# A two-layer graph kernel: first inputs of three pairs loaded at once, weights relaid, a replanned order

## The chip, the cores and the metric

The kernel runs on one core of a Trainium2 chip. TensorE (PE in the profile) multiplies matrices, VectorE (DVE) and ScalarE (ACT) work elementwise, GpSimd (POOL) does a few small operations, and SyncE (SP) issues nearly all transfers (DMA). Each engine takes its instructions in the order in which the program holds them, and waits on semaphores for what other engines or transfers must have finished. The metric is the device time of one execution in microseconds (us), lower is better. Before the change three runs took 2926.58, 2936.07 and 2936.2 us, median 2936.07 us.

## The reference, cut to what matters

There are 64 graphs of 256 nodes with 256 features each; everything is float32. Layer 0 is twice a graph attention, then a feed-forward part; layer 1 is an attention with 8 heads whose weights are masked by relation, then a feed-forward part.

```python
def gat(h, adj, W, a):                       # layer 0, twice
    Wh = h @ W
    e = leaky_relu(Wh @ a[:256] + (Wh @ a[256:]).T, 0.2)
    return softmax(where(adj > 0, e, NEG), axis=1) @ Wh
h = layernorm(x + gat(gat(x, ...), ...))
h = layernorm(h + relu(h @ w_ff1 + b_ff1) @ w_ff2 + b_ff2)
q, k = h @ Wq + bq, h @ Wk + bk              # layer 1, 8 heads of 32
attn = softmax(q @ k.T / sqrt(32))
out = sum((attn * (adj == r)) @ (h @ Wv[r] + bv[r]) for r in range(4))
h = layernorm(h + out @ Wo + bo)
return layernorm(h + gelu(h @ W1 + b1) @ W2 + b2)
```

## The kernel before

Two graphs make a pair, and 32 pairs run through the same way (`whole_way`, a generator): the two graph attentions (`gat_layers`), feed-forward, attention, feed-forward, store. Several pairs are in flight at once. The order of all instructions is made by a planner while the program is written, in `run`. It keeps a clock for each engine, takes the next step of a generator when TensorE's clock says that its inputs, its PSUM banks (eight) and its buffers are there, and queues the work of the other engines through `put`, which gives it a duration, a `lag` until others may read its result, and a rank. `keep_order` then fixes that order for each engine. So a planned duration changes no instruction; it changes where each one stands in its engine's queue. `START` gives the clocks at which the planner lets each engine begin, `landed` when it believes groups of weights to have arrived, and `CHANGES` changes ranks, degrees and orders at set times of TensorE's clock. `HURRIED` pairs (the first two) turn their attention rows by TensorE instead of through DRAM.

The start is written by hand. The lines up to L191 fold the two weight matrices of graph attention into `w12`: DVE forms four columns (L181), TensorE multiplies, and DVE copies the two halves out. `load` then brings a pair's three inputs: `xT` (512 KB, for the first product), `adjT` (512 KB of integers, made bytes by ACT at L390 and reduced by DVE at L394) and `x` (512 KB, for the residual). Pair 0 comes before the weights and pair 1 behind the first feed-forward weights. Their `adjT` lie in the buffer of the later values `v`; both pairs' `xT` share the one buffer `input`, and so does every transfer of a later pair's `xT` and `adjT`, so that pair 2's `adjT` waits for pair 1's first product, and its `xT` for that `adjT` to be read.

In `gat_layers` a first product (L166 over `input`) gives `xw`, which ACT evacuates (L650); ACT makes exponentials (L582 to L584), TensorE turns them into rows (L595) that ACT copies (L598); DVE weighs with the adjacency (L630, L632, one instruction each per half graph); ACT scales `xw` by the reciprocal sums (L639), and TensorE aggregates (L166 over `xw,e`). This is done twice. The name `gat` is held by one pair until its second product is done, so the next pair's first product waits for that.

Between these, `reliefs` takes the constant parts of biases out of the weights: one-column products (L1170) for the first feed-forward, for q and k, and for the second feed-forward, and then sums of weight blocks on DVE (L446, L440), since many products are done in seven block products instead of eight. These need the weights, which arrive in 28 transfers for six large matrices alone, cut as the blocks are used, in runs of 512 bytes to 2 KB.

Of the kernel before, what the change touches and what calls it, by code (L numbers as in the profile page):

```python
# [26 lines left out]
HURRIED = 2  # L27
SEVEN = (0, 2)
# [3 lines left out]
    (27.0, ("all", "slack", 0.2), ("rank", "means", 0)),  # L32
    (117.0, ("rank", "means", 1)),
    (207.0, ("all", "qkv", ("a1", "b1", "b2", "a2", "a6", "a5", "b6", "a7", "a4", "b5", "b7", "a3", "b4", "s0", "b3", "s1")),
     ("rank", "adj", 1), ("rank", "normalise", 2), ("rank", "exp", -1)),
    (297.0, ("degree", "fill", 1), ("all", "groups", (([0], []), ([1], []), ([], [2]), ([], [3]), ([2], []), ([3], []))),
     ("degree", "first", -1), ("all", "slack", 0.3)),
    (387.0, ("degree", "fill", 2.5), ("all", "slack", 0.8), ("rank", "mask", 1.5), ("rank", "turn", 2),
     ("all", "first", ("a1", "b1", "a6", "a2", "b2", "b6", "a5", "a7", "b7", "a4", "b5", "b4", "a3"))),
    (477.0, ("all", "slack", 0.1)),  # L40
    (657.0, ("rank", "qk", 2), ("rank", "adj", 0), ("rank", "act", 0.5), ("rank", "last", 0.5)),
    (1197.0, ("rank", "invert", 1.5), ("rank", "adj", -1), ("rank", "exps", -0.5),
     ("all", "first", ("a1", "b1", "a2", "a6", "b2", "b6", "a5", "a7", "b7", "a4", "b5", "b4", "a3")),
     ("rank", "normalise", 0), ("degree", "rows", 2)),
    (1287.0, ("rank", "turn", 1)),
    (1377.0, ("all", "groups", (([0], []), ([1], []), ([], [2]), ([], [3]), ([2], []), ([3], []))), ("rank", "divide", 1.5),
     ("rank", "copies", -2), ("all", "flight", 5)),
    (1467.0, ("all", "first", ("a1", "b1", "a2", "a6", "b2", "b6", "a5", "a7", "b7", "b5", "a4", "b4", "a3")),
     ("rank", "addends", 0.5)),
    (1557.0, ("rank", "copies", 1), ("rank", "qk", -2)),  # L50
    (1827.0, ("rank", "copies", -2)),
    (1917.0, ("rank", "v", 1)),
    (2007.0, ("rank", "rows", 1.5), ("rank", "squares", -0.5), ("rank", "copies", 0)),
    (2367.0, ("rank", "last", 1), ("rank", "adj", -0.5), ("degree", "attention", 0)),
    (2547.0, ("rank", "divide", 1), ("rank", "mask", 3)),
    (2637.0, ("degree", "first", 2.5)),
    (2727.0, ("rank", "last", 3), ("rank", "second", 0.5)),
    (2817.0, ("all", "first", ("a1", "b1", "a2", "a6", "b2", "b6", "a5", "a7", "b7", "b5", "a4", "b4", "a3")),
     ("rank", "second", -0.5), ("rank", "rows", -2)),
# [12 lines left out]
START = {"tensor": 8.5, "vector": 8.0, "scalar": 4.0, "gpsimd": 0.0, "sync": 32.0}  # L72
# [3 lines left out]
def two_layers(ctx: ExitStack, tc: tile.TileContext, t: dict, out: bass.AP, flag: bass.AP):  # L76
# [98 lines left out]
    nc.sync.dma_start(right[:, :, :D], t["L0_gnn_W2"].rearrange("(c p) m -> p c m", p=P))  # L175
    nc.scalar.dma_start(a2, bass.AP(tensor=t["L0_gnn_a2"].tensor, offset=t["L0_gnn_a2"].offset, ap=[[0, P], [1, 2 * D]]))
    nc.sync.dma_start(w1T, t["L0_gnn_W1T"].rearrange("(c p) m -> p c m", p=P))
# [7 lines left out]
    for columns in (slice(0, D), slice(D, D + 4)):  # L185
        for m in range(KC):
            for c in range(KC):
                by_strips(both[m][:, columns], lhsT=w1T[:, c, m * P:(m + 1) * P], rhs=right[:, c, columns],
                          start=c == 0 and columns.start == 0, stop=c == KC - 1, skip_group_check=True)
    for m in range(KC):  # L190
        nc.vector.tensor_copy(w12[:, m], both[m][:, :D + 4])  # L191
# [15 lines left out]
    free = {name: [0.0] * n for name, n in (("bank", 8 - KEPT), ("kept", KEPT), ("a", HQ), ("m", HQ), ("h", HQ), ("yb", 1), ("yT", 2), ("yTa", 1),  # L207
# [15 lines left out]
    def put(engine, us, emit, *events, rank=1, lag=0.2, kb=0, function=None, needs=None, frees=(), event=None, behind=None):  # L223
# [46 lines left out]
    def took(us):  # L270

        clock["tensor"] += us
        return at_time(clock["tensor"] + 0.2)
# [14 lines left out]
    def run(besides, ways):  # L288
# [12 lines left out]
        while True:  # L301
# [42 lines left out]
            else:  # L344
# [6 lines left out]
                clock[engine] += piece["us"]  # L351
# [15 lines left out]
    def load(pair, at=None):  # L367
# [4 lines left out]
        def adjT():  # L372
            if at is not None:
                to["adjT"] = work.tile([P, 2, 2, 2 * D], F32, name="v")[:, pair].bitcast(I32).rearrange(
                    "p b (c n) -> p (b c) n", c=2)
            else:
                to["adjT"] = io.tile([P, 4, N], I32, name="input")
            nc.sync.dma_start(to["adjT"], t["adjT"][rows].rearrange("b (c p) n -> p (b c) n", p=P))

        def xT():  # L380
            to["xT"] = io.tile([P, KC, 512], F32, name="input")
            nc.sync.dma_start(to["xT"], t["xT"][pair].rearrange("(c p) b n -> p c (b n)", p=P))
# [20 lines left out]
        if at is None:  # L403
            adj = in_bytes(there(adjT, needs="input"))
            return to, [there(xT, adj), adj, there(x, needs="x")]
        takes("input", pair == 0)
        takes("x")
        for emit in (xT, adjT, x):
            emit()
        return to, [at_time(at), in_bytes(at_time(at)), at_time(at)]  # L410

    def first_weights(name, wide=None):

        w = t[name]
        rows = w.shape[1] // 2
        s = const.tile([P, 7, rows], F32, name="w_" + name)
        for c, at in ((0, (0, 2)), (1, (1, 6))):
            for half, n in enumerate(at):  # L420
                nc.sync.dma_start(s[:, n], w[c * P:(c + 1) * P, half * rows:(half + 1) * rows])
# [9 lines left out]
    def last_weights(name):  # L431

        s = const.tile([P, 7, NF // 2, P], F32, name="w_" + name)
        for c, h, at in ((1, 0, 0), (0, 0, 1), (0, 1, 2), (1, 1, 3)):
            nc.sync.dma_start(s[:, at], t[name][c * FF // 2:(c + 1) * FF // 2, h * P:(h + 1) * P].rearrange("(k p) d -> p k d", p=P))
        return s

    def last_sums(w, there, event):
        for to, a, b in ((4, 3, 0), (5, 2, 4), (6, 2, 3), (3, 1, 5)):
            there = put("vector", 0.6, lambda to=to, a=a, b=b: nc.vector.tensor_tensor(w[:, to], w[:, a], w[:, b], ALU.subtract),  # L440
                        there, rank=5, event=event if to == 3 else None)
# [203 lines left out]
    def gat_layers(pair, to, loads):  # L645
        yield loads[:1], ["gat"], 2
        y = work.tile([P, 4, D + 4], F32, name="xw", bufs=2)
# [15 lines left out]
        frees_at(clock["tensor"], ["input"] * (pair > 0))  # L663
# [3 lines left out]
        for b in range(2):  # L667
            yield [e[b][1], *([] if b or not pair else [through_gat[pair - 1]])], None, 2
            if b == 0:
                z = work.tile([P, 4, D + 4], F32, name="xw", bufs=2)  # L670
# [7 lines left out]
        done_with("gat")  # L678
# [3 lines left out]
        for b in range(2):  # L682
# [7 lines left out]
            frees_at(there.time, ["e"])  # L690
# [437 lines left out]
    def layernorm_weights(g, beta, more=None):  # L1128
# [5 lines left out]
        return on_all(g, D), on_all(beta, D), more  # L1134

    landed = {name: at_time(us) for name, us in (("ln0", 8.0), ("ff0", 15.0), ("attention", 30.0), ("ff1", 37.0))}
    loaded = {0: load(0, 6.5)}
    ln = [layernorm_weights("L0_gnn_g_ln1", "L0_gnn_b_ln1", "L0_gnn_b_ff2")]
    ff0 = (first_weights("L0_gnn_w_ff1p"), column("L0_gnn_b_ff1"), (last_weights if 0 in SEVEN else weights)("L0_gnn_w_ff2"), Event())
    loaded[1] = load(1, 18.0)  # L1140
    ln.append(layernorm_weights("L0_gnn_g_ln2", "L0_gnn_b_ln2", "L1_gnn_bo"))

    wqk, wv = (const.tile([P, 7, D], F32, name=n) for n in ("wqk", "wv"))
    for n, name in enumerate(("L1_gnn_Wqp", "L1_gnn_Wkp")):
        for half, c, at in ((0, 0, 0), (0, 1, 1), (1, 0, 2), (1, 1, 6)):
            nc.sync.dma_start(wqk[:, at, n * P:(n + 1) * P], t[name][c * P:(c + 1) * P, half * P:(half + 1) * P])
    for r, c, at in ((0, 0, 0), (0, 1, 1), (1, 0, 2), (1, 1, 6)):
        nc.sync.dma_start(wv[:, at], t["L1_gnn_Wvp"][r, c * P:(c + 1) * P, :])
    bqk = const.tile([P, 2, KC], F32, name="bqk")
    for n, name in enumerate(("L1_gnn_bq", "L1_gnn_bk")):  # L1150
# [3 lines left out]
    ln.append(layernorm_weights("L1_gnn_g1", "L1_gnn_beta1", "L1_gnn_b2"))  # L1154
    ff1 = (first_weights("L1_gnn_W1p"), column("L1_gnn_b1"), (last_weights if 2 in SEVEN else weights)("L1_gnn_W2"), Event())
    ln.append(layernorm_weights("L1_gnn_g2", "L1_gnn_beta2"))
    biased = [put("vector", 0.4, lambda gbm=gbm: nc.vector.tensor_tensor(gbm[1], gbm[1], gbm[2][0], ALU.add), landed[name])
              for gbm, name in zip(ln, ("ln0", "attention", "attention"))]
    differences = [put("vector", 0.4, lambda to=to, of=of: nc.vector.tensor_tensor(to, to, of, ALU.subtract), landed["attention"])
                   for to, of in ((wv[:, 2], wv[:, 0]), (wv[:, 6], wv[:, 1]), (bv[:, D:], bv[:, :D]))]  # L1160
    relieved, through_gat = [Event() for _ in range(3)], [Event() for _ in range(NPAIR)]
# [21 lines left out]
    def reliefs():  # L1183
# [3 lines left out]
        if 0 in SEVEN:  # L1187
            last_sums(ff0[2], relieved[0], ff0[3])
# [13 lines left out]
        if 2 in SEVEN:  # L1202
            last_sums(ff1[2], relieved[2], ff1[3])
# [427 lines left out]
_BY_TRANSPOSED_ROWS = ("L0_gnn_w_ff1", "L1_gnn_Wq", "L1_gnn_Wk", "L1_gnn_Wv", "L1_gnn_W1")  # L1631
_ROWS_AND_COLUMNS = ("L0_gnn_b_ff2", "L1_gnn_bo", "L1_gnn_b2")

# [30 lines left out]
```

## Time and profile before

| | |
|---|---|
| median of three runs | 2936.07 us |
| the profiled execution's own time | 2928.64 us |
| its span in the profile | 2926.9 us |
| TensorE busy | 2874.6 us, 98% |
| DVE busy | 2629.6 us, 90% |
| ACT busy | 1847.4 us, 63% |
| mean granted TensorE clock | 0.993 |
| transfers | 211.84 MB, 72 GB/s on average |

The profile's rows by stretch of time give, for each engine, its busy microseconds and how many instructions these were; `PEclk` is the share of full clock granted to TensorE, and `DMA share` how busy the 16 transfer engines were. A row of the timeline has start, duration, engine, line, operation and tiles, and in brackets how long the engine had stood idle and what ended it. A matmul row's count is twice the program's for float32 data[...]. `PEld` is the load of the stationary operand.

### The profile page before, as it was taken

The numbers are of one execution on the slowest core, as the hardware profiler recorded it, in microseconds if no ns is written. First come the engines' busy times: TensorE is split into PE (matmuls) and PEld (weight loads), VectorE is DVE, ScalarE is ACT, GpSimd is POOL, SyncE is SP. The second block draws the span as 40 slices with busy tenths as digits, with TensorE's granted clock in tenths as the row PEclk, the third lists the DMA queues.
The fourth block names the chain that finished last, engine by engine and source line by source line (L and its number), as shares of the span: only waits on it lengthen the run. The fifth ranks groups of instructions, "written<-read, shape, count | busy, mean of one in ns | idle before, by whom it ended". The sixth has DMA issues, their size and how long they took to land. (4 is left out here: it accounts for less than half of the span.)

```text
span 2926.9 us, 147784 instructions
## 1 busy us (share of the span) xinstructions
PE 2874.6 (98%) x66066; PEld 2062.1 (70%) x66066; DVE 2629.6 (90%) x5874; ACT 1847.4 (63%) x5120; POOL 274.1 (9%) x518
## 2 busy tenths in 40 slices
PE   7999999999999999999999999999999999999998
PEld 4766776776776667766777767678767788677676
DVE  6899999899998889989998998999999999998887
ACT  4667666657656566565666665666666666665655
POOL 0010000100100001010100010010010000110001
PEclk8999999999999999999999999999999999999999
DMA  6222212222212222122222222221222222222100
GB/s 190 68 74 79 68 53 79 85 85 61 79 60 71 84 66 82 59 76 82 71 72 69 74 82 76 67 79 64 82 75 81 66 78 68 77 73 65 36 10 25
DMA packets 214178, 211.84 MB, mean 72 GB/s; under 512 B 22944, under 2 KB 173088, under 8 KB 213536
## 3 DMA queue, kind: packets, MB, share of 16 engines
q1 hardware_dynamic: 213120, 202.06, 22.0%
q8 instruction: 520, 8.52, 1.2%
q14 instruction: 122, 1.00, 0.1%
q10 hardware_dynamic: 416, 0.26, 0.0%
HBM read 137.51 MB, written 64.73 MB: 69 GB/s over the span
## 5 line engine op out<-in xcount | busy, mean ns | idle before, releaser
L166 PE MATMUL ps<-w_L_gnn_w_ff,ff 128*32 128x128 f32 x14336 | 426.9, 273 | 2.1 <-issue 1.4
L166 PEld LDWEIGHTS ps<-w_L_gnn_w_ff,ff 128*32 128x32 f32 x14336 | 397.3, 110 | 36.3 <-issue 13.0
L166 PE MATMUL ps<-w_L_gnn_W,ff 128*32 128x128 f32 x14336 | 418.3, 273 | 2.2 <-DVE qk L1091 0.9
L166 PEld LDWEIGHTS ps<-w_L_gnn_W,ff 128*32 128x32 f32 x14336 | 393.8, 110 | 30.6 <-issue 5.6
L1046 ACT ACTIVATE a<-ps 128x512 f32<-128x512 f32 x512 | 265.8, 600 | 145.7 <-PE ps L1037 145.0
L166 PE MATMUL ps<-yT,w_L_gnn_w_ff1p 128*32 128x256 f32 x5120 | 321.4, 382 | 10.8 <-ACT xw L650 10.6
L920 DVE TENSOR_TENSOR ff<-ff 128x1024 f32<-128x1024 f32 x256 | 311.2, 1215 | 16.0 <-PE ps L166 12.6
L738 POOL TENSOR_SCALAR rstd<-squares 128x2 f32<-128x2 f32 x256 | 78.2, 306 | 2625.1 <-ACT unread L733 2622.5
L733 ACT ACTIVATE unread<-x,less 128x256 f32<-128x256 f32 x512 | 259.6, 507 | 99.6 <-DVE less L708 68.6
L166 PE MATMUL ps<-yT,w_L_gnn_W1p 128*32 128x256 f32 x5120 | 316.0, 379 | 1.3 <-ACT ff L845 0.5
L845 ACT ACTIVATE ff<-ps 128x512 f32<-128x512 f32 x384 | 221.7, 588 | 146.5 <-PE ps L166 145.1
L1050 DVE TENSOR_TENSOR m<-a,adj 128x1024 f32<-128x1024 f32 x256 | 306.0, 1215 | 1.0 <-ACT a L1046 1.0
L517 DVE TENSOR_TENSOR ff<-ps,ff 128x512 f32<-128x512 f32 x384 | 260.2, 682 | 31.9 <-PE ps L166 20.4
L166 PE MATMUL ps<-xw,e 128*32 128x258 f32 (+1 forms) x4096 | 248.9, 385 | 5.8 <-ACT xw L639 5.8
L166 PEld LDWEIGHTS ps<-yT,w_L_gnn_w_ff1p 128*32 128x32 f32 x5120 | 172.6, 110 | 113.6 <-ACT xw L650 13.5
L166 PEld LDWEIGHTS ps<-yT,w_L_gnn_W1p 128*32 128x32 f32 x5120 | 171.9, 110 | 100.1 <-ACT ff L845 5.7
L851 ACT ACTIVATE ff<-ff,c_L_gnn_b_ff 128x256 f32<-128x256 f32 x384 | 172.8, 502 | 101.5 <-DVE ff L517 101.0
L917 DVE TENSOR_TENSOR x<-ps,x 128x256 f32<-128x256 f32 (+1 forms) x384 | 191.8, 504 | 33.8 <-PE ps L166 30.4
L166 PEld LDWEIGHTS ps<-xw,e 128*32 128x32 f32 x4096 | 138.4, 111 | 90.7 <-ACT xw L639 8.5
L739 POOL TENSOR_TENSOR rstd<-rstd,mhalf 128x2 f32<-128x2 f32 x256 | 195.2, 763 | 21.3
L851 ACT ACTIVATE ff<-ff,c_L_gnn_b 128x256 f32<-128x256 f32 x384 | 172.3, 504 | 36.8 <-DVE ff L517 35.5
L1007 ACT ACTIVATE qk<-ps,bqk 128x256 f32<-128x256 f32 x256 | 109.3, 468 | 118.3 <-PE ps L166 117.3
(133 smaller groups left out, 5091.7 us busy)
## 6 DMA issues: line engine op xcount, KB each, us to landing
home<-yb SPq DMA_DIRECT2D x182, 256.0 KB, 2.2
yT<-home SPq DMA_DIRECT2D x728, 64.0 KB, 2.1
rows<-row SPq DMA_DIRECT2D x60, 512.0 KB, 4.1
input<-in_xT SPq DMA_DIRECT2D x32, 512.0 KB, 3.8
x<-in_x SPq DMA_DIRECT2D x32, 512.0 KB, 3.9
out<-x SPq DMA_DIRECT2D x64, 256.0 KB, 2.6
input<-in_adjT SPq DMA_DIRECT2D x30, 512.0 KB, 3.9
v<-in_adjT SPq DMA_DIRECT2D x2, 512.0 KB, 7.1
```

The source lines that it names most:

```text
L166: nc.tensor.matmul(to[at:at + DH], lhsT=lhsT[:, at:at + DH], rhs=rhs, **flags)
L517: nc.vector.tensor_tensor(self.target(*where), self.bank["z"], self.target(*where), ALU.add)
L733: nc.scalar.activation(unread, rows[j], AF.Square, bias=of["less"][:, j:j + 1], accum_out=squares[:, j:j + 1])
L738: nc.gpsimd.tensor_scalar(rstd, squares, 1.0 / D, EPS, ALU.mult, ALU.add)
L739: nc.gpsimd.tensor_tensor(rstd, rstd, mhalf[:, :2], ALU.pow)
L845: return put("scalar", 0.5, lambda: nc.scalar.activation(target(c, h), of, AF.Copy), event, rank=rank_of["copies"])
L851: evacuated[h][m] = put("scalar", 0.4, lambda m=m, to=to, source=source: nc.scalar.activation(to, source, func, bias=b1[:, m:m + 1]), even ...
L917: return put("vector", us, lambda: nc.vector.tensor_tensor(to, of, to, ALU.add), *events, rank=rank_of["last"], frees=frees)
L920: return put("vector", 1.14, lambda: nc.vector.tensor_tensor(to, a, b, op), *events, rank=rank_of["sums"])
L1007: nc.scalar.activation(target_qk(c, b)[:, n], of[:, n], AF.Identity, bias=bqk[:, n, c:c + 1])
L1046: nc.scalar.activation(a[n][q][:, k], ps[2 * q + k], AF.Exp)
L1050: nc.vector.tensor_tensor(m[n][q], a[n][q], adj, ALU.mult)
```

## The change

Six things are done together.

1. `xT` and `adjT` of three pairs are loaded early (`EARLY = 3`), each into a buffer of its own: `xT` of pair 1 and 2 into the two halves of `qk`, the three `adjT` into buffers `m`, all needed only later for attention. SP issues pairs 0 and 1 right behind `W2`, pair 2 behind the first feed-forward's first weights, and the pairs' `x` later. `W1T` moves to ACT's queue, ahead of `a2`.
2. `gat` is no longer held by one pair. Two `xw` buffers are counted instead, pair 1's first values lie in `v`, and a pair may begin its first product once the pair before has begun its second.
3. Weights and layer norm constants are laid out on the host so that they come in long runs: the 28 transfers become 10, and each two layer norm vectors one.
4. `w12` is made half by half, the second half copied by ACT.
5. The planner's `lag` goes from 0.2 to 0.3 us, DVE's planned durations are raised by 3%, and `START`, `LANDED` and `THERE` hold new times.
6. `CHANGES` is replaced by another list (20 entries for 22).

In the program as built, the counts of arithmetic instructions are the same, but for one copy moved from DVE to ACT. ACT has 122 table loads instead of 72, with the path for other inputs that doesn't run counted in both. SP has 1265 transfers instead of 1288, one of them now ACT's.

```diff
-START = {"tensor": 8.5, "vector": 8.0, "scalar": 4.0, "gpsimd": 0.0, "sync": 32.0}
+START = {"tensor": 9.5, "vector": 9.3, "scalar": 9.7, "gpsimd": 0.0, "sync": 36.0}
+LANDED = (("ln0", 15.0), ("ff0", 18.5), ("ff0_last", 26.0), ("ln1", 28.5), ("attention", 34.5), ("ff1", 40.0), ("ff1_last", 43.0))
+THERE = ((6.5, 8.0, 13.5), (9.5, 11.0, 27.5), (20.5, 22.0, 35.0))
...
+    nc.scalar.dma_start(w1T, t["L0_gnn_W1T"].rearrange("(c p) m -> p c m", p=P))
     nc.scalar.dma_start(a2, bass.AP(tensor=t["L0_gnn_a2"].tensor, offset=t["L0_gnn_a2"].offset, ap=[[0, P], [1, 2 * D]]))
-    nc.sync.dma_start(w1T, t["L0_gnn_W1T"].rearrange("(c p) m -> p c m", p=P))
...
-    for columns in (slice(0, D), slice(D, D + 4)):
-        for m in range(KC):
+    for m in range(KC):
+        for columns in (slice(0, D), slice(D, D + 4)):
...
-    for m in range(KC):
-        nc.vector.tensor_copy(w12[:, m], both[m][:, :D + 4])
+    nc.vector.tensor_copy(w12[:, 0], both[0][:, :D + 4])
+    nc.scalar.activation(w12[:, 1], both[1][:, :D + 4], AF.Copy)
...
-    def put(engine, us, emit, *events, rank=1, lag=0.2, kb=0, function=None, needs=None, frees=(), event=None, behind=None):
+    def put(engine, us, emit, *events, rank=1, lag=0.3, kb=0, function=None, needs=None, frees=(), event=None, behind=None):
...
-                clock[engine] += piece["us"]
+                clock[engine] += piece["us"] * (1.03 if engine == "vector" else 1.0)
...
-        for c, at in ((0, (0, 2)), (1, (1, 6))):
-            for half, n in enumerate(at):
-                nc.sync.dma_start(s[:, n], w[c * P:(c + 1) * P, half * rows:(half + 1) * rows])
+        nc.sync.dma_start(s[:, :3], t[name + "m"][:, :3])
+        nc.sync.dma_start(s[:, 6], t[name + "m"][:, 3])
...
-        yield loads[:1], ["gat"], 2
-        y = work.tile([P, 4, D + 4], F32, name="xw", bufs=2)
+        yield [loads[0], *([z_begun[pair - 1], through_gat[pair - 2]] if pair > 1 else [])], None, 2, *(["xw"] * (pair != 1))
+        y = in_values if pair == 1 else work.tile([P, 4, D + 4], F32, name="xw", bufs=2)
...
+    homes = [work.tile([P, 2, 512], F32, name="m", bufs=HQ).rearrange("p b (c n) -> p (b c) n", c=2) for _ in range(EARLY)]
+    homes = list(zip((io.tile([P, KC, 512], F32, name="input"), of_qk[:, 0], of_qk[:, 1]), homes))
...
+    for pair in range(2):
+        emit[pair][0]()
+        emit[pair][1]()
+    emit[0][2]()
+    ln = [layernorm_weights("ln0", "L0_gnn_b_ff2")]
+    ff0 = [first_weights("L0_gnn_w_ff1p"), column("L0_gnn_b_ff1")]
+    emit[2][0]()
+    emit[2][1]()
+    ff0 += [last_weights("L0_gnn_w_ff2"), Event()]
+    emit[1][2]()
```

## The prediction

> **What bounds the kernel now.** I read first the busy times and the slices, then stretches of time, then who TensorE waited for, and at last the timeline of the start. The page:
>
> ```profile
> PE 2874.6 (98%) x66066; PEld 2062.1 (70%) x66066; DVE 2629.6 (90%) x5874; ACT 1847.4 (63%) x5120; POOL 274.1 (9%) x518
> PEclk8999999999999999999999999999999999999999
> ```
>
> TensorE bounds it: 98% busy at full clock, but for the first slice. No edit removes a product, so the change can only win back time that TensorE stands idle or runs slow. The stretches show where that lies:
>
> ```profile
> 0.00:10.00 10.00, 2.93 (x32) 1.61 (x36) 2.04 (x14) 1.28 (x1) 0.68 (x6) 1.00 0.69 220
> 20.00:30.00 10.00, 4.58 (x39) 2.72 (x43) 4.83 (x11) 3.04 (x6) 0.00 (x0) 0.51 0.84 254
> 40.00:50.00 10.00, 7.38 (x84) 3.39 (x85) 7.18 (x30) 1.81 (x4) 0.00 (x0) 0.66 1.03 320
> 50.00:60.00 10.00, 8.58 (x111) 7.49 (x113) 9.59 (x31) 6.27 (x17) 2.50 (x4) 0.71 0.35 116
> 80.00:1340.00 1260.00, 1245.34 (x28716) 880.59 (x28712) 1141.96 (x2548) 803.30 (x2227) 118.87 (x222) 1.00 0.23 72
> 1340.00:2870.00 1530.00, 1524.46 (x35268) 1107.02 (x35263) 1399.67 (x3084) 983.14 (x2717) 144.63 (x272) 1.00 0.22 69
> ```
>
> After the length come the busy times of PE, PEld, DVE, ACT and POOL, then the granted clock. Between 80 and 2870 us TensorE idles 14.7 + 5.5 = 20.2 us; 80:1340 and 800:890 taken closer show two dips to 0.98 over 90 us, 3.6 us more: 24 us. The first 63 us are worse. Up to 62.7 us TensorE has done 35.6 us of work at full clock (added from rows: 3.5 for a pair's first product or aggregation, 4.0 for a one-column product of a feed-forward, 1.1 for rows, 0.86 per eight products), so it loses 27 us there. The timeline shows the largest piece:
>
> ```profile
> 17.26 3.96 PE L1170 MATMUL ps<-c_L_gnn_b_ff2c,w_L_gnn_w_ff1p 128*128 128x1 f32 x30 [0.38 <-DMA w_L_gnn_w_ff1p<-in_L_gnn_w_ff1p]
> 25.12 1.06 ACT L390 ACTIVATE adj<-v 128x1024 uint8<-128x1024 int32 x1 [7.77 <-DMA v<-in_adjT]
> 26.63 5.51 PE L166 MATMUL ps<-xw,e 128*32 128x258 f32 x64 [5.42 <-ACT xw L639]
> 44.55 5.07 PE L166 MATMUL ps<-xw,e 128*32 128x256 f32 x64 [0.40 <-ACT xw L639]
> ```
>
> Pair 1's `adjT` lands at 25.1, and ACT, in order, waits for it with pair 0's scaling (L639) queued behind, though DVE's reciprocals were ready at 19.9. TensorE waits for that scaling, and then runs the 64 matmuls in 5.51 us that take 3.45 at full clock.
>
> **The start, step by step.** The changed order on TensorE is: `w12`; pair 0's first product; pair 1's; pair 0's rows; first relief; pair 1's rows; pair 0's aggregation; half of pair 1's; pair 0's second rows; the other half; q, k, v relief; second feed-forward relief; pair 0's second aggregation; pair 1's rows; pair 2's first product; transposes; half of pair 1's second aggregation. I walk it with durations of the trace.
>
> `w12`: `W1T` no longer follows `W2` on SP, but `a2` now follows `W1T` on ACT's queue, and DVE's four columns wait for it (landing near 7.0 instead of 5.8, by the bytes moved up to then). Halves save one copy (0.38): ready at 10.6 against 11.05. Both first products, 2 x 3.5: 17.6; pair 1's inputs, fourth and fifth on SP, land near 10.5 and 12, where 2.2 and 2.7 MB had been moved before. Pair 1's product, at 31.97 and 34.85 before, now covers pair 0's exponentials. Rows 1.1: 18.7. Relief 4.0: 22.7, needing weights moved by then (18.5 by bytes). Pair 1's rows: 23.8.
>
> Meanwhile ACT copies rows (1.21, 19.3), DVE does three weighings of 0.97 (the order has one of the second graph between) and a reciprocal: 21.8 to 22.1. ACT again has an `adjT` ahead of the scaling: pair 2's, by bytes at 21 to 22, read by 23.1. Scaling 0.9: aggregation at 24.0, against 26.63. If that transfer is 4 us late, so are pair 0's scaling, TensorE behind it and pair 1's rows on ACT: the price of this wait is its lateness, one for one.
>
> Then pair 1: rows copied 25.2; DVE has block sums, pair 2's reduction (1.4) and one bias sum that waits for layer norm constants (near 29) before its reciprocal: 31; scaling 32. TensorE, done at 27.5 to 29, idles some 3 us. Two halves and rows (1.75 + 1.1 + 1.75, or 2.75 for a half at low clock): 37 to 38. Reliefs 2.0 + 1.7 to 2.9 + 4.0: 45 to 46; their weights (near 34.5 and 40) come in time. Pair 0's second aggregation, with its scaling ready at 42: 3.5 to 5.1, 48.5 to 51. Rows, pair 2's product, transposes and a half: 1.1 + 3.5 + 2.1 + 1.75, so 56.6 to 59.6. The work done by then is 35.6 + 7.2 = 42.8 us, so 13.8 to 16.8 us are lost, against 27.1: gain 10.3 to 13.3.
>
> *Rule and row on the clock.* The clock fell to half at 20.1 us, while the relief's one-column products ran from 17.26 to 21.2 and TensorE was listed as busy; so it did at 54.3 behind the other relief. The Trainium skill, page "TensorE: Matmul & The Clock Gate", Part 1, says that an idle window of about 3.4 us halves the clock, and a busy window restores it. It speaks against the change, which keeps one real gap (28 to 32): half of one window, 1.7 us, gain 11.6. By the rows the reliefs count as idle too: the two aggregations at 5.51 and 5.07 for 3.45, together 3.7 us less than 13.3, gain 10. I take 11. The low end is 6 (pair 2's `adjT` four late), the high end 13.
>
> **Weights in long runs.** Between 27 and 30 us, eight 64 KB and then 128 KB transfers were moved at 101 to 140 GB/s with the engines 35 to 62% busy: SP's issues (0.33 to 0.45 each) set that. At 21 to 24 us `xT` and `adjT` moved at 366 to 379 GB/s. From 18 to 20 us, when the second matrix was in flight in 512-byte runs, it was 214 to 227 at a share of 0.81 to 0.97. The Trainium skill, page "DMA: Bandwidth & Descriptors", section Specifications, puts the minimum transfer for line rate at 512 B: by it the long runs gain nothing for that 1 MB, by the row 1 MB goes from 4.7 to 2.8 us. Either way the last weights land near 43 instead of 48 to 49. I add nothing: the reliefs' places in TensorE's order hide it, and weights 5 us later (the old arrival) would stop the second relief by 3 to 5 us, which the range holds.
>
> **The rest of the run.** New lags, a 3% longer DVE, another `CHANGES` and the freer `gat` reorder all pairs. They add no product. The waits that they could take away:
>
> ```profile
> PE ps L166 <- ACT xw L650: 10.6, 5, 3.2
> PE ps L166 <- ACT ff L845: 1.7, 2, 1.4
> PE ps L166 <- issue: 1.7, 3, 1.1
> ```
>
> Half of the 20.2 us is five waits behind one ACT evacuation; at 885 us ACT had first stood 2.9 us for a transposed transfer. A lag larger by 0.1 sets users further back, but doesn't lengthen planned transfers. No row shows the new order, so I bound it: all of it won, -24; or as much again lost, +24. I take -9, a little over a third, since the last 1530 us before show that such an order can lose only 5.5.
>
> What speaks against it is ACT's table loads:
>
> ```profile
> L851 ACT ACT_TABLE_LOAD x35 | 44.9, 1283 | 0.6
> L582 ACT ACT_TABLE_LOAD x19 | 24.4, 1283 | 0.3
> L1046 ACT ACT_TABLE_LOAD x15 | 19.2, 1283 | 2.1 <-PE ps L1037 1.9
> ```
>
> 70 loads become 120: 64 us more on ACT, which idles 1080. In the repeated part of the new order, the exponentials of the third group of scores are followed by a load, two gelus, another load and those of the fourth group. Four exponentials take 2.4; those of the fourth start 6.1 us after the third scores and end by 8.4; masks and halves on DVE (3.6) end near 12, and TensorE takes the fourth products at 5.0 + 11.7 = 16.7 (11.7 being what the order puts between). Cover 4.7, cost nothing; with the cover gone 1.28 a pair.
>
> At the end the new order puts the last pair's third products 4.1 us behind their scores, and its fourth 4.75; exponentials, halves and masks took 6.2 at 839.6 to 845.8. So TensorE waits 2.1 + 1.5, say 4, where the old order had 12.3 between. The last 12 us stay.
>
> **The sum.** -11 - 9 + 4 = -16 on a profiled execution of 2928.64 us (span 2926.9): 2912.6. The median shown lies 7.4 above that execution, and I keep the distance: 2936.07 - 16 = 2920.
>
> **The rivals.** (a) *Only the start gains*: new stalls equal the old, -11 + 4, less 0 to 5 for late weights or `adjT`: 2929 to 2934. For it: the lag of transfers is unchanged, and the long waits came from one. Against: more margin everywhere else. (b) *The order closes nearly all stalls*: -11 - 24 + 4 = -31, 2905. For it: the quiet second half. Against: other ranks at other times. (c) *Slower, by table loads*: 1.28 us for each of 26 pairs is +33, less 11 and plus 4: 2962. It decides when the masks of the fourth group come over 4.7 us later than I have them, which DVE, 90% busy, could do if the third group's masks queue behind other work. (d) *The early loads do nothing*, as ACT waits for pair 2's `adjT` as it did for pair 1's: gain 6 in place of 11, inside (a).
>
> **How the numbers follow.** The sum as worked 0.50, with its own range 2908 to 2930; (a) and (d) 0.28; (b) 0.12; (c) 0.10. About 0.5% (14.7 us, below 2921.4) is what a measurement of this kernel can tell from no change. Of the first, three quarters lie beyond it: 0.38 + 0.12 = 0.50 faster; 0.12 + 0.28 = 0.40 within; 0.10 slower. The range 2899 to 2946 leaves out (c) and the better part of (b)'s far side.
>
> **What would show it.** Right: pair 1's first product before 18 us, aggregation at 23 to 25, TensorE's five-microsecond stretches full from 57 to 60 on; idle from 80 to 2850 below 20 us; about 120 table loads without TensorE waiting behind them; some 4 us idle among the last pair's third and fourth products. Wrong: a wait of over 2 us for pair 2's `adjT`, a clock of half to 50 us, or an equal stall in every pair near the third and fourth products.

## The result, and the profile after

The kernel after takes 2900.28 us (median; 2898.27 to 2902.55), beside 2936.2 us (2926.58 to 2944.82) for the kernel before on the same chip. The ratio is 0.9877, with a 95% interval from 0.9854 to 0.9899. The predicted time was 2920 us with a range of 2899 to 2946: the direction was right and the time lies just inside the edge of the range, but the gain is 36 us where the sum gave 16.

The profiled execution took 2901.78 us (span 2900.0), 26.9 us less span than before. The other 9 us are not in the two profiles at all: the median before lies 7.6 us above its profiled execution, the median after 1.5 below its own. From the page of the kernel after, the busy times:

```profile
PE 2862.7 (99%) x66066; PEld 2038.1 (70%) x66066; DVE 2636.5 (91%) x5873; ACT 1910.2 (66%) x5171; POOL 285.3 (10%) x518
```

TensorE idles 37.3 us of the span where it idled 52.3. Its busy time is 11.9 us shorter for the same 66066 matmuls, and the mean granted clock is 0.997 where it was 0.993. The rows by stretch (columns as before):

```profile
20.00:30.00 10.00, 10.00 (x108) 7.49 (x104) 7.34 (x21) 6.79 (x20) 0.00 (x0) 0.83 0.98 338
40.00:50.00 10.00, 10.00 (x113) 7.33 (x116) 6.93 (x26) 2.87 (x7) 0.00 (x0) 0.84 0.59 207
80.00:1340.00 1260.00, 1252.34 (x29076) 903.06 (x29072) 1162.25 (x2584) 833.42 (x2268) 122.15 (x224) 1.00 0.24 74
1340.00:2843.00 1503.00, 1496.81 (x34592) 1052.97 (x34588) 1381.92 (x3038) 1004.73 (x2708) 152.28 (x268) 1.00 0.22 68
```

From 20 to 30 us and from 40 to 50 us TensorE is now full, and the clock there is 0.83 and 0.84 in place of 0.51 and 0.66. From 80 to 1340 it idles 7.7 us where it idled 14.7; from there to the last pairs 6.2 (5.5 before). What it still waits for:

```profile
PE ps L163 <- DMA a<-in_L_gnn_W1T: 4.7, 1, 4.7
PE ps L163 <- DMA xw<-in_L_gnn_a1c: 3.8, 1, 3.8
PE ps L1060 <- ACT a L1038: 3.5, 2, 3.0
PE ps L163 <- DMA yT<-home: 3.1, 1, 3.1
```

The five waits behind the evacuation (L650 before, L641 now), 10.6 us, are gone from the list.

To see where in the run the time came from, I added up TensorE's work to a moment, every matmul at the full-clock time that the traces show for its shape (54.0 ns for 128x256, 27.3 for 128x128, 111 for one column), and compared the moments at which equal work was done. Other prices for a shape move a gain by 0.2 us at most. The last column is an experiment below.

| us of the span of before | gain of the kernel after | gain of the kernel before with no wait for `yT` |
|---|---|---|
| 63 | 10.1 | -1.7 |
| 80 | 8.9 | -1.7 |
| 260 | 10.4 | 1.1 |
| 350 | 5.5 | 1.6 |
| 884 | 7.4 | -0.8 |
| 1340 | 25.0 | 11.6 |
| 2420 | 30.3 | 13.1 |
| 2840 | 29.8 | 13.4 |
| 2870 | 24.5 | 13.4 |
| end of the span | 26.9 | 13.0 |

So the start is worth 8.9, the run from 80 to 2840 another 20.9 (most of it, 17.6, between 884 and 1340), and the end gives 2.9 back. The sum had 11, 9 and 4. One execution's start differs from the next: in three more profiles with the start of the kernel after (a_noyT, a_noload, a_late, all below) the gain at 80 us is 8.6 to 10.7, and in two with the start of the kernel before (b_noyT, b_late) it is -1.7 and -0.9.

### The profile page after: what moved, and what is told of

Same layout as the page of the kernel before. It is cut to its first block, busy times and chain, and to the rows that moved or that the text cites. A ratio compares the mean times of both kernels' runs of the same rounds, so it can differ in the third digit from the quotient of the medians.

```text
span 2900.0 us, 147819 instructions
## 1 busy us (share of the span) xinstructions
PE 2862.7 (99%) x66066; PEld 2038.1 (70%) x66066; DVE 2636.5 (91%) x5873; ACT 1910.2 (66%) x5171; POOL 285.3 (10%) x518
## 4 chain that ended last, share of the span: by engine, by line
PE 93%; DVE 3%; DMA 2%; ACT 1%; issue 0%; SPq 0%; ACTq 0%; DVEq 0%; POOL 0%; POOLq 0%
PE ps L163 79%; PE ps L1060 7%; PE ps L1029 4%; PE ps L1063 2%; DMA yT<-home 0%; DVE ff L912 0%; DVE m L1042 0%; DVE x L739 0%; DMA home<-yb 0%; DMA b_ln<-in_ln 0%; DMA w_L_gnn_w_ff1p<-in_L_gnn_w_ff1pm 0%; DMA xw<-in_L_gnn_a1c 0%; DVE h L1046 0%; DVE x L736 0%; DVE ff L508 0%
## 5 line engine op out<-in xcount | busy, mean ns | idle before, releaser
L163 PE MATMUL ps<-w_L_gnn_W,ff 128*32 128x128 f32 x14336 | 424.2, 273 | 0.6 <-ACT a L1038 0.4
L163 PE MATMUL ps<-yT,w_L_gnn_W1p 128*32 128x256 f32 x5120 | 305.8, 380 | 3.2 <-DMA yT<-home 3.1
L163 PE MATMUL ps<-yT,w_L_gnn_w_ff1p 128*32 128x256 f32 x5120 | 306.4, 379 | 0.0
L163 PE MATMUL ps<-xw,e 128*32 128x256 f32 (+1 forms) x4032 | 245.5, 383 | 1.3 <-ACT xw L630 1.3
L163 PEld LDWEIGHTS ps<-yT,w_L_gnn_W1p 128*32 128x32 f32 x5120 | 165.7, 110 | 106.0 <-ACT ff L837 6.8
L736 DVE SCALAR_TENSOR_TENSOR x<-x,less,b_ln 128x256 f32<-128x256 f32 x512 | 227.5, 478 | 7.3 <-ACT unread L725 6.6
L739 DVE SCALAR_TENSOR_TENSOR x<-x,rstd,b_ln 128x256 f32<-128x256 f32 x512 | 229.4, 479 | 1.3 <-POOL rstd L731 1.3
L909 DVE TENSOR_TENSOR x<-ps,x 128x256 f32<-128x256 f32 (+1 forms) x384 | 193.9, 505 | 21.4 <-PE ps L163 16.2
L731 POOL TENSOR_TENSOR rstd<-rstd,mhalf 128x2 f32<-128x2 f32 x256 | 205.7, 803 | 21.3
```

Source lines behind the costliest of these rows:

```text
L163: nc.tensor.matmul(to[at:at + DH], lhsT=lhsT[:, at:at + DH], rhs=rhs, **flags)
L731: nc.gpsimd.tensor_tensor(rstd, rstd, mhalf[:, :2], ALU.pow)
L736: nc.vector.scalar_tensor_tensor(rows[j], rows[j], of["less"][:, j:j + 1], g, op0=ALU.add, op1=ALU.mult)
L739: nc.vector.scalar_tensor_tensor(rows[j], rows[j], rstd[:, j:j + 1], beta, op0=ALU.mult, op1=ALU.add)
L909: return put("vector", us, lambda: nc.vector.tensor_tensor(to, of, to, ALU.add), *events, rank=rank_of["last"], frees=frees)
```

## The experiments

### What stalled the kernel before from 884 to 1340 us

The timeline of the kernel before, engines together:

```profile
870.44 2.78 SPq L791 DMA_DIRECT2D yT<-home  x4
873.32 0.38 SPq L785 DMA_DIRECT2D home<-yb  x1
877.48 1.73 SPq L791 DMA_DIRECT2D yT<-home  x4
...
882.13 0.63 ACT L973 ACTIVATE yTa<-yT 128x512 f32<-128x512 f32 x1 [2.93 <-DMA yT<-home]
...
887.14 0.64 ACT L650 ACTIVATE xw<-ps 128x258 f32<-128x258 f32 x2
...
887.56 3.38 PE L166 MATMUL ps<-yT,w_L_gnn_w_ff1p 128*32 128x256 f32 x32 [3.23 <-ACT xw L650]
```

A pair's rows are transposed by DVE, stored to DRAM (`home<-yb`) and gathered again (`yT<-home`, four transfers). Here SP is busy with one half's four issues until 873.2, so the other half's store, whose data DVE had ready at 871.98, goes out at 873.32; with the first gather in flight beside it, it is there only at 877.4. Its own gather lands near 882. ACT stands 2.93 us for it, with eight other activations queued behind, and the evacuation that TensorE needs is the ninth, at 887.14. TensorE idles 3.23 us and runs the next 32 matmuls in 3.38 us that take 1.9 at full clock. The engine that the list of TensorE's waits named, ACT, had itself waited for a transfer.

To weigh that cause alone, ACT's copy of the transposed rows reads the rows before their transposition, which have long been there, in both kernels; no instruction changes its place.

```diff
             nc.scalar.activation(yT[:, b].rearrange("p c (k a i) -> p (c k) a i", k=2, a=4),
-                                 normal["yT"][:, b].rearrange("p a (ck i) -> p ck a i", i=32), AF.Copy)
+                                 y[:, 2 * b:2 * b + 2, :].rearrange("p b (x a i) -> p (b x) a i", x=2, a=4), AF.Copy)
```

> The kernel before, its order of instructions unchanged, but ACT's copy of a pair's transposed rows in one piece (yTa) reads the layer-normed rows themselves and not what the transposed transfer brought, so ACT no longer waits for that transfer (attention is computed from untransposed rows; the output is not the reference's). Theory A (the 16 to 18 us that the kernel before loses against the one after between 880 and 1340 us come from ACT standing in its queue for the transposed transfer, with an evacuation behind it): 10 to 20 us faster than before, TensorE's waits for the evacuation L650 (10.6 us, 5 times) gone or under 3 us. Theory B (the transfer is only where the wait shows; DVE or banks hold the same places): within 5 us of before, and other waits of about 10 us in their stead.

> The same edit in the kernel after, its order unchanged (output not the reference's). Theory A (the new order has already got out of the way of these transfers): at most 6 us faster than the kernel after, ratio to before 0.985 to 0.988. Theory B (the new order lives with as many stalls for the transfer, and gains elsewhere): 10 us faster or more, ratio below 0.984.

Measured: in the kernel before 2916.76 us against 2935.54, ratio 0.994 (0.9924 to 0.9957), 18.8 us less. In the kernel after 2897.98 us, ratio to before 0.9873 (0.9856 to 0.989), 2.3 us less than its own median. TensorE's waits from 870 to 1340 us in the kernel before:

```profile
PE ps L166 <- ACT xw L650: 10.2, 4, 3.2
```

and with ACT's wait taken away, waits and timeline:

```profile
PE ps L166 <- DVE ff L517: 0.6, 1, 0.6
PE ps L166 <- ACT xw L650: 0.2, 1, 0.2
...
880.01 0.62 ACT L973 ACTIVATE yTa<-x 128x512 f32<-128x512 f32 x1
...
885.43 1.93 PE L166 MATMUL ps<-yT,w_L_gnn_w_ff1p 128*32 128x256 f32 x32 [0.22 <-ACT xw L650]
```

Theory A held in both kernels: in the kernel before, one repeated wait of ACT made most of these stalls. Of the 17.6 us that the kernel after wins between 884 and 1340, the take-away wins 12.4 in the kernel before (last column of the table), and 15.1 of the 20.9 between 80 and 2840. With the wait away in both, the kernels are still 18.8 us apart (2916.76 and 2897.98): about half of the 36 us goes with that wait, and the rest is the start and some 10 us of the later run.

The take-away also narrows the times: 2914.82 to 2922.16 (six executions) with the wait gone, 2929.13 to 2945.12 (eleven) for the kernel before on the same chip; and its median lies 1.1 us above its own profiled execution, where that of before lay 7.6 above. So the stalls seem to differ from one execution of the kernel before to the next. A second trace with the order of before (b_noadj, below) agrees: it loses 7.0 us less between 884 and 1340.

Does the new order leave these transfers room, or has it only fewer bad places? Three transfers of 2 KB ahead of each half's gathers delay them, again with no instruction of another engine moved.

```diff
+        spares = lambda: [nc.sync.dma_start(r, home[:1]) for r in (next(spare), next(spare), next(spare))]
...
         def gather():
-            if b == 0:
+            if spares() and b == 0:
```

> The kernel before, its order on TensorE, DVE, ACT and GpSimd unchanged, with three transfers of 2 KB that nobody reads ahead of each half's four gathers: SP issues these gathers 1.3 us later (three issues of 0.43). Theory A (in this order many pairs' ACT and TensorE already stand for the transposed transfer, 55.8 us and 32 times on ACT): 10 to 40 us slower, ratio 1.003 to 1.014, with more of TensorE's waits behind the evacuation L650. Theory B (the stalls between 880 and 1340 were a few odd places): under 6 us.

> The same three small transfers in the kernel after, its order unchanged. If the new order leaves these transfers room (slack and list together): under 5 us slower than after, ratio to before at most 0.9895. If it has no more room than the old order and only its transfers come earlier: as many us slower as the kernel before becomes, 10 to 40, ratio 0.991 or more.

Measured: 3067.1 us for the kernel before with the delay, ratio 1.0463 (1.0435 to 1.0491), and 3001.32 us for the kernel after, 1.0238 (1.021 to 1.0267): 135 and 101 us for a delay that, from a store's issue to its gather's, is 1.9 and 2.0 us in the median. I had the size wrong for both. ACT and TensorE in the kernel before with the delay:

```profile
ACT yTa L973 <- DMA yT<-home: 138.5, 48, 6.9
PE ps L166 <- ACT xw L650: 29.4, 6, 5.4
```

and in the kernel after with it:

```profile
ACT yTa L965 <- DMA yT<-home: 78.6, 26, 8.0
PE ps L163 <- DVE v L1005: 38.3, 17, 4.8
```

Before, ACT stands 138.5 us for the transfer, after 78.6, and TensorE now waits for DVE's sums rather than for that evacuation. So the new order has a little more room, and neither has 2 us of it. The three issues also put SP's other transfers off; that was not separated.

### Lag, slack and list by themselves

Four kernels undo or do one part, with the list left as it was or exchanged: the kernel after with the old list and without slack (s_only), with the old list alone (s_k), without slack alone (s_c), and the kernel before with a longer planned gather, so that ACT's copy is placed later (b_gather).

The slack is the planner's larger `lag` and DVE's 3%. The edit of b_gather:

```diff
-        to[b] = put("sync", 1.75, gather, there, *([to[0]] if b else []), lag=1.7, kb=64, needs=None if b else "yT")
+        to[b] = put("sync", 1.75, gather, there, *([to[0]] if b else []), lag=4.7, kb=64, needs=None if b else "yT")
```

> The changed kernel with the old list of changes, a lag of 0.2 and DVE's durations without the 3%: only the start, the layout and the freer first layers are new. If the start's gain carries to the end and the rest comes from list and slack: 8 to 11 us faster than before, with waits of TensorE behind an evacuation left somewhere between 80 and 1400 us. If the freer first layers are what removed the later stalls: 25 to 36 us faster, as the whole change. If the old list fits only the old start: equal or up to 20 us slower, as its entries now meet the wrong moments.

> As the one with only the start, plus the slack: lag 0.3 and DVE 3% longer in the plan, still with the old list. If the slack brings the later gain: 25 to 36 us faster than before. If it is the new list: no more than 5 us from the run with the start alone.

> As the one with only the start, plus the new list of changes, but with the old lag and DVE's plain durations. If the list brings the later gain: 25 to 36 us faster than before. If the list and the slack belong together (the list made for that lag): 0 to 15 us faster.

> The kernel before with one planned number changed: the lag of the four transfers that gather a transposed half is 4.7 us in place of 1.7, so that ACT's copy of it, and all that uses it, stands later in the queues. No transfer and no operation is added. Theory that the old order loses its time because ACT waits for that transfer with an evacuation queued behind (five waits of TensorE, 10.6 us, and 4 to 8 us of low clock after them): 10 to 20 us faster, TensorE's wait for the evacuation (L650) down from 10.6 to under 3 us, ACT's wait for the transfer (55.8 us) under 20. Rival, that the waits come from other places of that order: within 5 us of before. Rival, that a longer planned way leaves too little to do: slower.

All four are slower than the kernel before (2930.05 us on that chip): 3037.22, 3135.06, 2955.8 and 2972.49 us, ratios 1.0354, 1.0692, 1.0078 (1.0052 to 1.0105) and 1.0145. In b_gather ACT's waits for `yT` did fall, from 55.8 to 1.0 us, and others took their place. In the kernel after with the old list:

```profile
PE ps L169 <- DVE qk L1089: 62.2, 15, 14.3
```

A list of rank changes at set times of the planner's clock belongs to one plan. Moved under another lag or another start, its entries can hit other pieces. These runs can't be read as the worth of a part. No list at all (`CHANGES = ()`) in four kernels takes that confusion away, though each is still only one order; a fifth run puts the new list and the slack together on the old structure.

> The kernel before with an empty list CHANGES: the planner's defaults throughout. Its order fits nothing in particular, so nothing is out of fit. If the fitted list hides 50 us or more: 2980 to 3020, ratio 1.015 to 1.03. If the planner's own order is nearly as good: below 2960.

> The kernel before with an empty list, and the slack in the plan (lag 0.3, DVE 3% longer). If slack makes any order more robust against late transfers: 15 us or more faster than the kernel before with an empty list. If slack is worth something only together with a list fitted to it: within 10 us of it, or slower.

> The kernel after without slack (lag 0.2, DVE at its measured durations) and with an empty list: the early loads, long runs and freer first layer alone. If the start's 8 us are all that these are worth: 8 us faster than the kernel before with an empty list, give or take 10 for another order. If the freer first layer also helps every later pair: 20 us faster or more.

> The kernel after with an empty list: structure and slack. If slack and structure add up on their own: 20 to 30 us faster than the kernel before with an empty list, and within 40 us of the kernel after. If the gain lies in the fitted list: 60 us or more slower than the kernel after (above 2960), and no nearer to it than the kernel before with an empty list is to the kernel before.

> The kernel before with the new list and the slack in the plan, and with its old start, old loads, weights and first layer. If list and slack are worth something without the structure they were fitted to: 10 to 25 us faster than before, ratio 0.991 to 0.997. If the list fits one exact plan only, as the kernel after with the old list says: slower than before by 25 to 100 us.

| without a list | without slack | with slack |
|---|---|---|
| structure before | 3016.79 | 3070.93 |
| structure after | 3049.43 | 3085.07 |

Without a list the slack costs 54 and 36 us, and the new structure costs 33 and 14: in these orders neither is worth anything by itself past the start. The old list is worth 83 us on its plan, the new one 185 on its own. List and slack on the old structure (k_c) give 3070.76 us, ratio 1.0474 (1.0447 to 1.0501). So the gain past the start was seen only with list, slack and structure together, and no run shows a gain from the slack's margin by itself.

### The start

The prediction read the wait for pair 1's `adjT` as the largest piece of the start. In the kernel before, pair 1's adjacency is made from a tile that is already there, in two ways; the order stays.

```diff
-            nc.scalar.activation(to["adj"], to["adjT"], AF.Copy)
+            nc.scalar.activation(to["adj"], first.bitcast(I32) if pair == 1 else to["adjT"], AF.Copy)
...
-            nc.vector.tensor_reduce(most[:, pair], to["adjT"].bitcast(U32), axis=AX.X, op=ALU.max)
+            nc.vector.tensor_reduce(most[:, pair], (first if pair == 1 else to["adjT"]).bitcast(U32), axis=AX.X, op=ALU.max)
```

> The kernel before, its order unchanged, with pair 1's adjacency made bytes and reduced from pair 0's tile, which is there, so that ACT doesn't wait 7.77 us for pair 1's adjT (pair 1's output is not the reference's). If that wait sets the start as the timeline was read: pair 0's aggregation at 21.5 to 22.5 in place of 26.63, and 4 to 6 us gained from there to the end of the span. If the start is held elsewhere too (weights, half clock): the aggregation is early and the gain at 63 us is under 2.

> The kernel before, its order unchanged, with pair 1's adjacency made bytes and reduced from pair 0's x, which is there, so that nothing waits for pair 1's adjT and SP's queue is not held (pair 1's output is not the reference's). If that wait was the start's largest piece: aggregation at about 22.4, SP's weights as early as before, q, k, v relief done by about 42 as before or earlier, and 3 to 5 us gained at 63 us of the span. If the weights that land at 41 us hold the start by themselves: the aggregation 4 us early, and at 63 us under 2 us gained.

With pair 0's `adjT` as the source (b_noadj; the diff shows the other way, where `first` is pair 0's `x`), the time is 2934.18 us, ratio 1.0008 (0.9995 to 1.0021): nothing. But the edit let SP wait for DVE's reading of that buffer before it issued pair 1's `adjT`, at 23.90 in place of 18.84 us, so that all weights behind it came later too, and at 63 us of the span 5.0 us were lost. With pair 0's `x` as the source (b_noadj2) SP's queue is as early as before. There pair 1's adjacency is so unlike the real one that the kernel takes its path for other inputs after the usual one, so its whole time (10604.43 us) says nothing; the first 63 us of its timeline do:

```profile
20.76 5.38 PE L166 MATMUL ps<-xw,e 128*32 128x258 f32 x64 [0.27 <-ACT xw L639]
...
42.23 0.43 DVE L1157 TENSOR_TENSOR b_L_gnn_beta<-b_L_gnn_beta,ff 128x256 f32<-128x256 f32 x1 [11.91 <-DMA c_L_gnn_b<-in_L_gnn_b]
...
43.05 1.93 PE L166 MATMUL ps<-wv,c_L_gnn_boc 128*32 128x256 f32 x16 [9.38 <-DVE wv L1159]
```

The aggregation comes 5.9 us earlier, and at 63 us nothing is gained (-0.9): TensorE then waits 9.38 us in place of 2.53. DVE stands 11.91 us with a bias sum (L1157) for layer norm constants that SP brings behind all the attention weights, and the small sums of `wv` (L1159), which TensorE needs, are queued behind it. Two waits held the start of the kernel before, and the first hid 7 us of the second. The change removed both; in the kernel after DVE's rows are

```profile
37.40 0.75 DVE L1165 TENSOR_TENSOR wv<-wv 128x256 f32<-128x256 f32 x2
...
43.90 0.42 DVE L1163 TENSOR_TENSOR b_ln<-b_ln,ff 128x256 f32<-128x256 f32 x1
```

because the third bias sum is now planned for the second feed-forward's landing (`"ff1"` where `"attention"` stood, in the line of `biased`): it stands behind the sums of `wv`. By these rows that one word is part of the start's gain, and my walk passed over it; no run changes it alone.

The walk's own times, in the kernel after:

```profile
10.41 2.31 PE L163 MATMUL ps<-xw,a 128*32 128x4 f32 x48 [3.77 <-DMA xw<-in_L_gnn_a1c]
...
12.54 5.40 PE L163 MATMUL ps<-w,input 128*32 128x260 f32 x64
...
27.26 4.84 PE L163 MATMUL ps<-xw,e 128*32 128x258 f32 x64
34.18 1.95 PE L163 MATMUL ps<-v,e 128*32 128x258 f32 x32 [2.08 <-ACT v L630]
...
42.69 3.73 PE L1176 MATMUL ps<-c_L_gnn_b2c,w_L_gnn_W1p 128*128 128x1 f32 x32
```

Folded weights were to be ready at 10.6; TensorE waits for a 2 KB transfer, `a1c`, until 10.41 and is ready 2 us late. Is that transfer's place the reason? It is issued first instead of third:

```diff
+    nc.scalar.dma_start(right[:, :, D + 2:], t["L0_gnn_a1c"])
     nc.scalar.dma_start(w1T, t["L0_gnn_W1T"].rearrange("(c p) m -> p c m", p=P))
     nc.scalar.dma_start(a2, bass.AP(tensor=t["L0_gnn_a2"].tensor, offset=t["L0_gnn_a2"].offset, ap=[[0, P], [1, 2 * D]]))
-    nc.scalar.dma_start(right[:, :, D + 2:], t["L0_gnn_a1c"])
```

> The kernel after with the 2 KB transfer of four ready columns (a1c) issued first on ACT's queue and not third. TensorE's four-column products, which waited for it at 10.41 us, then wait for DVE's last of four columns, done at 9.65: first product of pair 0 at 11.8 in place of 12.54. If the small transfer alone held the folded weights, 0.7 to 1 us in the start and as much at the end, under what the ratio can tell (0.986 to 0.989); if pair 0's rows and not the folded weights set the start, nothing moves after 27 us.

2903.01 us, ratio 0.9889 (0.9872 to 0.9906): no gain. Its timeline:

```profile
6.59 1.93 PE L163 MATMUL ps<-xw,a 128*32 128x256 f32 x16 [6.59 <-DMA a<-in_L_gnn_W1T]
10.58 0.29 PE L163 MATMUL ps<-xw,a 128*32 128x4 f32 x8 [2.05 <-DVE h L178]
```

With the small transfer ahead `W1T` lands at 6.59 instead of 4.70, and `a2` behind it is later too: DVE's columns (L178) end at 10.99 instead of 9.65, and TensorE's four-column products start at 10.58 and 11.04 instead of 10.41. So moving the small transfer gains nothing: what one of the three wins on ACT's queue, another loses.

Last, the six large matrices in the old short runs, the order unchanged:

```diff
-        nc.sync.dma_start(s[:, :3], t[name + "m"][:, :3])
-        nc.sync.dma_start(s[:, 6], t[name + "m"][:, 3])
+        w = t[name]
+        for c, at in ((0, (0, 2)), (1, (1, 6))):
+            for half, n in enumerate(at):
+                nc.sync.dma_start(s[:, n], w[c * P:(c + 1) * P, half * rows:(half + 1) * rows])
```

> The kernel after, its order unchanged, with the six large matrices brought again in the old short runs and many transfers. If the long runs are hidden, as I added nothing for them: within 2 us of after, ratio 0.987 to 0.9885. If late weights stop the second relief: 3 to 5 us slower in the start and at the end.

2905.08 us, ratio 0.9911 (0.9884 to 0.9937), 4.8 us above the median after, with intervals that overlap; at 63 us of the span it is 2.5 us behind. The timeline shows where:

```profile
43.83 5.21 PE L1181 MATMUL ps<-c_L_gnn_b2c,w_L_gnn_W1p 128*128 128x1 f32 x30 [0.95 <-DMA w_L_gnn_W1p<-in_L_gnn_W1p]
48.97 5.22 PE L163 MATMUL ps<-xw,e 128*32 128x256 f32 x64
```

The second feed-forward's relief waits 1.7 us for its weights and falls to half clock while it runs, where with long runs it took 3.73 and ended at 46.4. At 2870 us the two profiled executions are level (gains of 24.4 and 24.5 over the kernel before), so the traces do not show the loss reaching the end.

### The table loads

```profile
L843 ACT ACT_TABLE_LOAD x60 | 77.0, 1283 | 1.0
L1038 ACT ACT_TABLE_LOAD x33 | 42.3, 1283 | 0.6
L573 ACT ACT_TABLE_LOAD x26 | 33.4, 1283 | 0.5
```

120 loads, as predicted. To price them all, the kernel after keeps its order and takes an exponential in the second feed-forward, so that no table changes:

```diff
-                        to, source, func, bias=b1[:, m:m + 1]), event, rank=rank_of["act"] + h, function=kind,
+                        to, source, AF.Exp if func == AF.Gelu else func, bias=b1[:, m:m + 1]), event, rank=rank_of["act"] + h, function=kind,
```

> The kernel after, its order unchanged, with the second feed-forward's gelu replaced by an exponential, so that about 119 of the 120 table loads of 1.28 us fall away (output not the reference's). If the loads lie beside TensorE's work, as no wait of TensorE behind them says: 0 to 6 us faster than after, ratio 0.985 to 0.988. If they cost 1.28 us for a pair, as the slower rival had it: 30 us faster or more, ratio 0.977 or less.

2900.17 us, ratio 0.9881 (0.9864 to 0.9898): 0.1 us. ACT's busy time fell by 145.3 us, and the median did not move. The Trainium skill, page "ScalarE: Activation LUTs", section "What ACT_TABLE_LOAD costs", puts a switch at about 2.66 us with its drain, twice the load's 1283 ns; in the kernel after the next activation starts 1.3 us after the load does (median of 119), with ACT idle for under 0.02 us ahead of it, so no drain shows here. Only the last pair is different. Between 2780 us and the end TensorE's 3.5 us for the last masked products (see the waits above) become

```profile
PE ps L1060 <- ACT a L1038: 1.1, 2, 0.7
```

without the loads, and the profiled execution's span is 3.3 us shorter than that of the kernel after.

## Why the prediction was wrong, step by step

**"The rest of the run", -9: this step failed, by its size.** Mechanism and bound were right: between 80 and 2840 us the gain was 20.9 of the 24 us that I had bounded. I took "a little over a third" by comparison with the quiet second half. What should have weighed more stood beside the rows that I showed: one cause behind the stalls. At 885 us I saw that ACT had stood 2.9 us for a transposed transfer, and did not ask how often. In the kernel before and in the one after it stood so

```profile
ACT yTa L973 <- DMA yT<-home: 55.8, 32, 5.7
ACT yTa L965 <- DMA yT<-home: 39.7, 17, 5.0
```

Taking that wait away in the kernel before is worth 18.8 us at the median, twice my term. The kernel after still has 17 of these waits, but taking them away wins only 2.3 us: they stand where TensorE hardly feels them. That the new list would do so can't be read off its entries, and the runs without it, or with it on another plan, show that it could as well have gone 25 to 200 us the other way. My bound of +24 for a worse order was too small.

**"I keep the distance" of 7.4 us between profile and median: failed, 9 us.** With ACT's wait gone the distance is 1.1 us, and in the kernel after -1.5, so it belonged at least in part to the stalls of the kernel before, which vary between executions. Part is chance: on five other occasions the median of the kernel before was 2930.05 to 2935.54, which is 1.4 to 6.9 above that profiled execution.

**The start, -11: 8.9.** The size held within what one execution's start differs from the next, but not each step did. The walk gave 10.3 to 13.3. Its 35.6 us of work by 62.7 us are 33.7 when each matmul has its full-clock price; the excess stands on both sides of the walk, so the gain doesn't change. Both first products ran back to back (12.54 to 21.4), pair 2's `adjT` was read at 23.39 without stopping anything, so rival (d) fell, and one gap remained (32.1 to 34.2, shorter than the 3 us worked out). But the folded weights came 1.9 us late, the aggregation at 27.26 and not 24.0, and the walk's last step ended near 61 and not at 56.6 to 59.6. The clock went as the rows said. In the kernel after, the first relief runs from 22.30 to 25.9 with no idle time before it, the third from 42.69 to 46.36:

```profile
22.30:25.90 3.60, 3.60 (x35) 3.60 (x34) 3.23 (x11) 2.43 (x8) 0.00 (x0) 1.00 1.08 376
26.50:29.50 3.00, 3.00 (x28) 1.50 (x30) 2.90 (x9) 2.27 (x8) 0.00 (x0) 0.50 0.82 257
47.00:50.00 3.00, 3.00 (x36) 1.54 (x32) 0.81 (x3) 0.00 (x0) 0.00 (x0) 0.50 0.52 175
```

Behind each the clock is at half, and the 64 matmuls there take 4.84 and 5.35 us for 3.45. The rule of the Trainium skill, page "TensorE: Matmul & The Clock Gate", Part 1, by which an idle window halves the clock, would have left both aggregations at full. And the wait that I read as the start's largest piece was worth nothing alone: the steps around it earned the term.

**Long runs, 0.** As a step of the start they were worth 2.5 us there; I had named that price (3 to 5 if the weights were late) and then let "the reliefs' places" hide it. They don't hide it in the start; at 2870 us the profiled executions are level.

**The tail, +4.** TensorE's wait was 3.5 us at the products named, and the equal-work count shows 5.3 us given back between 2840 and 2870, of which 2.4 came back by the end: 2.9 in all. Half of that stall was table loads, which I had counted apart: without them the same stretch gives back 2.6.

**The rivals.** (c), slower by table loads, fell: without the loads the median is the same. (a) fell by its size. (b), nearly all stalls closed, is the nearest, 2905; idle time from 80 to 2843 us is 13.9 us, under the 20 that I had set as the sign.

Still open: between 260 and 350 us the kernel after loses 5 us that it had won, 3.1 of them in one wait for a `yT` transfer, and from 350 to 2420 it wins 13 us more than the kernel before does without ACT's wait (24.8 and 11.5). That part was not taken apart; no single row carries it.

## What to carry to other kernels

When the chain of waits names one engine again and again, follow that engine's queue back to what it was itself waiting for, and count that wait over the whole run before pricing it; then price it by taking away what it waits for, with every instruction left in place. A wait found in a timeline is worth its length only if the next one is not hidden behind it: here the first 5.9 us of the start bought nothing, because a bias sum on DVE waited for constants that came later still. And the list fitted to one plan could not be divided here: single edits under it measured the misfit, 25 to 205 us above the kernel before, and not the edit.

## What the runs showed that I had not expected

About 2 us more between a store and its gather, three small transfers per half, cost 135 and 101 us in a kernel whose transfer engines are busy a quarter of the time. They add 6 KB to 512 KB per half, so the queue's time is the likelier reason than the bytes. A transfer of 2 KB issued ahead of one of 256 KB put the larger one's landing off by 1.9 us, to 6.59; in ten other profiles, which issue the larger one first, it landed at 4.50 to 4.86. And the spread of the times was a reading in itself: 16 us before (eleven executions), 7 with one wait gone (six), 4 after (five).
